# Flamingo stack on one core: order on VectorE in the first attention, seven products for half of the first values, order of values and additions in the last layer

## The chip, the cores and the metric

The kernel runs on one core of a Trainium2 chip. The core has five engines with a queue of instructions each: TensorE (PE in the profile: matrix products into PSUM; PEld is its loading of weights), VectorE (DVE), ScalarE (ACT), GpSimd (POOL) and SyncE (SP, which here issues DMAs). An engine works through its queue in order; between engines, semaphores order the work. The metric is the device time of one execution in microseconds. A measurement of this kernel can tell changes of about 0.5%.

## The reference

Four layers over x (2 batches of 256 tokens, width 256) with a context ctx (2 batches of 512 rows, width 256). Each layer adds a gated cross attention and a gated feed-forward network (FFN). What this change touches:

```python
x = x + tanh(g_xattn[0]) * L0_xattn(layernorm(x), ctx)      # softmax attention, 16 heads, no weights
x = x + tanh(g_ffn[0])   * L0_ffn(layernorm(x), W_up, W_gate, W_down)
x = x + tanh(g_xattn[1]) * L1_xattn(layernorm(x), ctx, Wq, Wk, Wv, Wo)
...
x = x + tanh(g_xattn[3]) * L3_xattn(layernorm(x), ctx, mask)
x = x + tanh(g_ffn[3])   * L3_ffn(layernorm(x), ...)        # router, top 2 of 8 experts with capacity, plus a shared MLP

def ternary_quant(w):                                       # the weights of L0_ffn
    scale = mean(abs(w)) + 1e-8
    return clip(round(w / scale), -1, 1) * scale
# L0_ffn: (silu(x @ Wu.T) * (x @ Wg.T)) @ Wd.T
# L1_xattn: v = ctx @ Wv, and so q and k; softmax(q k / sqrt(128)) v @ Wo
```

## The kernel before

All of it is one function, `flamingo`, over tiles of 128 partitions. Tokens come as four tiles n = 0..3 of 128, two of each batch. The tile framework gives each engine a queue and puts in the semaphores. It may set an instruction ahead of another one of the text; `inline` forbids that where the text's order is wanted. While the list `line` holds something, each VectorE instruction passed to `inline` stands behind the one before it; `pool_line` and `pe_line` do the same for GpSimd and TensorE. `behind(i, j, ...)` sets one instruction behind another on the same engine.

*First attention* (L442 to 550). A loop over s = 0..17 issues scores of step s and values of step s - 1: four steps for each token tile, that is two halves of the heads (i) by two halves of the context. After the values of a half of the heads, `l0_join` multiplies the result by a column of ones and zeros into `mixed` (i = 0, L473) or adds it there (i = 1, L475). When a tile is complete, TensorE exchanges neighbouring groups of 16 rows (`l0_exchange`, L479), and `l0_finish` makes the reciprocal (L485), divides and adds to x; `norm_stats` and `norm_apply` (L217 to L236) prepare the norm for the FFN, with two small GpSimd steps for the scale (L219, L220).

Between these stand parts of the ternary quantisation of the FFN's three matrices: `ternary_sum` (L339, the sum of magnitudes on VectorE), `ternary_scale`, `ternary_below` (L360, GpSimd, w < -scale/2), and `ternary_signs` (L367, VectorE, two halves of 1024 columns for each matrix). Before, the sum of the third matrix follows tile 0's statistics (step 6), and the signs of the three matrices follow the first join of tiles 1, 2 and 3 (steps 6, 10 and 14), each ahead of the second join of the same tile.

*First FFN* (`ternary_ffn`, L770). `norm_tiles(split, xn0)` transposes the four normalised tiles into PSUM buffers of the tag "tr" (there are two), and `split` takes each apart into an upper part (L778, L779) and a rest (L780). Eight chunks of the hidden width follow: for each, eight products with signs (gate and up, L277, two PSUM buffers of the tag "mm", of which there are four), silu on ScalarE (L804), a multiplication and a truncation on VectorE (L805, L372), the rest on GpSimd (L374), and, one chunk later, the product with the third matrix (`l0_down`, L793).

*Values of the next attention.* `l1_values_of(0, tiles)` (L558) multiplies each of eight tiles of context rows (four of each batch) with the value weights of the first group of four heads. Seven of them stand between the first attention and the FFN, the eighth behind `norm_tiles`. The other three groups use `seven_values`: two products of 2 x 2 blocks each with seven in place of eight block products. `batch_sums` (sums of context blocks over both batches) and `weight_sums` (sums of weight blocks) are made on GpSimd; `seven` (L604) is a generator that yields after the second, fourth and seventh product, each in an "mm" buffer or, for m1, m6, m7 and m4, a "tr" buffer; its additions are VectorE's, the copy of m1 ScalarE's. `next` on such a generator puts a part of it between other work; the loop over the heads does so.

*After the FFN* come the keys of the first two heads, the norm for the second attention, its transposes, and the heads.

*Last layer.* `l3_values(n, ...)` (four products) for each token tile, then its statistics; `l3_rows(n)` writes the normalised rows (L1544, VectorE) for the experts, and `l3_turned2(n)` transposes them (L1550) for the router's logits. GpSimd then scatters rows to the experts' slots (L1607), SyncE loads the slots (L1681), and the experts run (L1700, L1722).

*End.* `accs` are the products of the shared MLP, `rows` the routed results; `add_to_x` (L280) adds an `acc` times the gate, L1807 the rows, and `store` writes a tile (L1792).

Of the kernel before, what the change touches and what calls it, by code (L numbers as in the profile page):

```python
# [17 lines left out]
F32 = mybir.dt.float32  # L18
# [4 lines left out]
ALU = mybir.AluOpType  # L23
# [26 lines left out]
def flamingo(ctx: ExitStack, tc: tile.TileContext, a: dict, out: bass.AP):  # L50
# [202 lines left out]
    def tokens(t, n):  # L253
        return t[:, n // 2, :, n % 2 * P : (n % 2 + 1) * P]
# [105 lines left out]
            inline(nc.gpsimd.tensor_scalar(t, wi, sc[:, 2:3], None, ALU.is_lt), pool_line)  # L360
            below.append((wi, sc, t))

    def ternary_signs():
        for _ in range(2):
            wi, sc, t = below.popleft()
            signs.append(q4.tile([P, 1024], F32R, tag="q4", name="signs"))
            inline(nc.vector.scalar_tensor_tensor(signs[-1], wi, sc[:, 1:2], t, ALU.is_gt, ALU.subtract))  # L367

    def halves(hi, lo, v):

# [126 lines left out]
    for s in range(18):  # L497
        n = s // 4
        if s < 16:
            es[s] = l0_scores(n, s // 2 % 2, s % 2)  # L500
        if s < 2:

            in_turn(nc.tensor.matmul(busy, lhsT=ones, rhs=ones, start=True, stop=True))

        if s % 4 == 2 and n or s == 17:
            done = n - 1
            l0_exchange(mixed[done], acc[done, 1], done == 1)
        if 1 <= s <= 16:
            m, i, half = (s - 1) // 4, (s - 1) // 2 % 2, (s - 1) % 2
            if half == 0:  # L510
                acc[m, i] = ps_acc.tile([P, 2, D], F32, tag="acc", name="acc")
            l0_values(m, i, half, es.pop(s - 1), acc[m, i][:, 0, :])
        if s == 0:
            ternary_sum(l0_w[0])
            ternary_sum(l0_w[1])
        if s == 3:
            behind(nc.scalar.activation(tg, graw, AF.Tanh), exps[-3], "with the table of exponentials")
            p = acc[0, 0][:, 1, :]
            for w in range(2):
                in_turn(ternary_total(p[:, w : w + 1], w))  # L520
            for w in range(2):
                ternary_scale(p[:, w : w + 1])
            ternary_below(0)
            value_columns(1)
            queries([2], rest[:1])
        if s % 4 == 2 and n or s == 17:
            r = l0_finish(done, acc[done, 1], mixed[done], done == 1)
            stats[done] = norm_stats(done)
            if done == 0:
                ternary_sum(l0_w[2])  # L530
            inline(nc.gpsimd.tensor_add(all_t, all_t, sums.pop(0)), pool_line)
# [42 lines left out]
        return kT  # L574


    v_next = l1_values_of(0, range(7))

# [15 lines left out]
    def weight_sums(pool, tag, u, v):  # L594

        cols = u.shape[2]
        t = pool.tile([P, 4, cols], F32, tag=tag, name="wsum")
        nc.gpsimd.tensor_add(t[:, 0, :], v[:, 0, :], v[:, 1, :])
        nc.gpsimd.tensor_sub(t[:, 1, :], t[:, 0, :], u[:, 0, :])
        nc.gpsimd.tensor_sub(t[:, 2, :], u[:, 0, :], v[:, 0, :])  # L600
        nc.gpsimd.tensor_sub(t[:, 3, :], u[:, 1, :], t[:, 1, :])
        return t

    def seven(u, v_, s, ctx_of, product, view, out):  # L604
# [24 lines left out]
        m4 = one(v_, t4, True)  # L629
        nc.vector.tensor_add(c21, c21, m4)  # L630
        yield
# [55 lines left out]
    def seven_values(g):  # L687

        v = slab[:, 8 + 2 * (g % 2) : 10 + 2 * (g % 2), :].rearrange("p s (m c) -> p (s m) c", m=4)
        w = l1_w[g][2]  # L690
        u, z = (w[:, :, i * 256 : (i + 1) * 256] for i in range(2))
        s = weight_sums(q4, "q4", u, z)

        def product(dst, w, t):
            for j in range(2):
                nc.tensor.matmul(dst[:, j, :], lhsT=t[:, j * P : (j + 1) * P], rhs=w, start=True, stop=True)  # L696

        def two(m):
            return seven([u[:, k, :] for k in range(2)], z[:, 1, :], [s[:, i, :] for i in range(4)],
                         context_of(slice(2 * m * P, 2 * (m + 1) * P)), product, lambda t: t.rearrange("p (j c) -> p j c", j=2),  # L700
                         [[v[:, b * 4 + 2 * m : b * 4 + 2 * m + 2, i * 256 : (i + 1) * 256] for b in range(B)] for i in range(2)])

        return v, [two(m) for m in range(2)]

# [66 lines left out]
    def ternary_ffn():  # L771


        xs = [q4.tile([P, B, 2, 256], F32R, tag="q4", name="xs") for _ in range(2)]

        def split(n, tr):
            top = q1.tile([P, 2, P], F32, tag="q1", name="topx")
            nc.vector.tensor_scalar(top.bitcast(I32), tr.bitcast(I32), -4096, None, ALU.bitwise_and)  # L778
            nc.scalar.copy(tokens(xs[0], n), top)  # L779
            nc.vector.tensor_sub(tokens(xs[1], n), tr, top)  # L780

        norm_tiles(split, xn0)
        l1_values_of(0, [7])
        s2 = small.tile([P, 1], F32, tag="s2", name="s2", bufs=1)
        nc.vector.tensor_mul(s2, scales[1], scales[2])
        nc.vector.tensor_mul(s2, s2, gf(0))
# [7 lines left out]
                                     start=(c == 0 and i == 0), stop=(c == 7 and i == 1))  # L794

        ps = {}
        for c, _, ts in by_batch(FCH):
            if c not in ps:
                ps[c] = mm(), mm()
            for w, p in zip((0, 2), ps[c]):  # L800
                chain(p[:, ts], [(signs[w + k][:, c * P : (c + 1) * P], batch(h, k, ts)) for k in range(2) for h in xs])
            if ts.stop == T:
                s = q2.tile([P, T], F32, tag="q2", name="silu")
                nc.scalar.activation(s, ps[c][0], AF.Silu, scale=scales[0])  # L804
                nc.vector.tensor_mul(s, s, ps[c][1])  # L805
                h = q4.tile([P, 2, T], F32R, tag="q4", name="hT")
                halves(h[:, 0, :], h[:, 1, :], s)
                later(lambda c=c, h=h: l0_down(c, h), 1)
        flush()
        for dh in range(2):  # L810
            p = outs[dh]
# [22 lines left out]
    norm_tiles(lambda n, tr: nc.scalar.copy(tokens(xT, n), tr), xn)  # L834
# [69 lines left out]
    for g in range(4):  # L904
# [3 lines left out]
        for hl in range(4):  # L908
# [15 lines left out]
            for b in range(B):  # L924
                es, by_ones, t = l1_scores(b, qT, kT, h > 13)
                if todo:
                    next(todo)
                if extra and (h == 1 or h and b != h % 2):
                    next(extra)
                later(lambda b=b, hl=hl, v=v, es=es, by_ones=by_ones, t=t, oT=oT: l1_attend(b, hl, v, es, by_ones, t, oT), 1)  # L930
            if todo:
                next(todo)
# [626 lines left out]
    for b in range(B):  # L1559
# [242 lines left out]
    final(1)  # L1802
    store(1)
    for n in (2, 3):
        if n == 3:
            add_to_x(3, accs[1], gf(3))
        inline(nc.vector.tensor_add(x[:, n, :], x[:, n, :], rows[n][:, 0, :]))  # L1807
        store(n)
    line.clear()
    pe_line.clear()  # L1810
# [655 lines left out]
```

## Time and profile before

| | us |
|---|---|
| median of 3 runs | 573.84 |
| the three runs | 573.16, 573.84, 576.12 |
| profiled execution | 572.92 |
| its span, first to last instruction | 571.2 |

| stretch of the span (us) | what runs | PE busy | DVE busy | ACT busy | POOL busy |
|---|---|---|---|---|---|
| 20 to 28 | first attention | 8.00 | 7.36 | 6.59 | 7.32 |
| 28 to 36 | first attention | 6.30 | 7.43 | 5.44 | 7.54 |
| 36 to 44 | first attention | 8.00 | 7.53 | 6.70 | 5.76 |
| 44 to 53 | its end | 7.27 | 8.58 | 3.58 | 8.92 |
| 53 to 66 | values, transposes | 13.00 | 5.80 | 4.75 | 6.76 |
| 66 to 89 | first FFN | 23.00 | 11.05 | 12.08 | 10.35 |
| 94 to 98 | norm, transposes | 3.09 | 3.20 | 2.10 | 3.77 |

The granted TensorE clock was 0.999 of full speed. A matrix product in fp32 appears in the trace as two TensorE instructions; their ends are modelled and overlap, so the cost of a run of them is read from the distance of their starts. A line of the view of waits names engine, instruction and line, what was waited for, the sum of the waits in us, how many, and the longest. A line of the timeline has start, busy time, engine, line, operation, output and inputs, count, and in brackets the idle time before it with what ended it. A line of the chain has start, length, engine, output and line.

### The profile page before, as it was taken

How to read it: one execution, taken by the hardware profiler on the slowest of the kernel's cores; microseconds unless marked ns; L12 is line 12 of the kernel's file. 1: busy time of each engine (PE TensorE's matmuls, PEld its weight loads, DVE VectorE, ACT ScalarE, POOL GpSimd, SP SyncE). 2: the span in 40 equal slices, each digit the busy share in tenths (PEclk: the TensorE clock that was granted, in tenths of full speed). 3: DMA queues.
4: the chain of work that ended last, by engine and by line, in shares of the span. 5: the costliest groups of instructions: out<-in, count | busy, mean ns of one | idle time of the engine just before them, and what ended most of it. 6: DMA issues, size and time to landing. Idle time of an engine off the chain costs nothing.

```text
span 571.2 us, 8750 instructions
## 1 busy us (share of the span) xinstructions
PE 553.1 (97%) x3300; PEld 401.0 (70%) x3300; DVE 371.9 (65%) x744; ACT 178.7 (31%) x329; POOL 216.4 (38%) x368
## 2 busy tenths in 40 slices
PE   8988999999999999999999999999999999999996
PEld 6553675778788787887878786887775555884445
DVE  6998444677867888588885895675567434563323
ACT  5874543422222222123222221331323221432221
POOL 3787456626332464134342344702022001252151
PEclk9999999999999999999999999999999999999999
DMA  7904200002002100102032324272020899704013
GB/s 294 412 18 188 107 0 1 0 1 74 1 0 75 43 32 1 37 37 75 0 118 104 117 94 158 75 239 75 0 75 2 338 419 415 170 33 129 18 53 116
DMA packets 15528, 59.15 MB, mean 104 GB/s; under 512 B 2653, under 2 KB 5924, under 8 KB 11846
## 3 DMA queue, kind: packets, MB, share of 16 engines
q1 hardware_dynamic: 13430, 53.70, 25.7%
q0 software_dynamic: 1472, 4.28, 2.3%
q8 instruction: 28, 0.46, 0.3%
q10 hardware_dynamic: 576, 0.53, 0.3%
q14 instruction: 22, 0.18, 0.1%
HBM read 53.70 MB, written 5.25 MB: 103 GB/s over the span
## 4 chain that ended last, share of the span: by engine, by line
PE 84%; DVE 8%; POOL 3%; issue 2%; ACT 1%; DMA 1%; SPq 0%; POOLq 0%; DVEq 0%; ACTq 0%
PE mm L277 22%; PE acc L277 18%; PE mm_t L646 4%; PE mm L658 4%; PE mm L1369 4%; PE mm_t L696 4%; PE mm L646 3%; PE mm_t L658 3%; PE mm L696 3%; PE acc L766 2%; PE s L450 2%; PE mm L1700 2%; PE acc L1390 2%; PE acc L1722 2%; PE acc L464 2%
## 5 line engine op out<-in xcount | busy, mean ns | idle before, releaser
L854 ACT ACTIVATE e<-mm 128x512 f32<-128x512 f32 x64 | 38.0, 597 | 115.0 <-PE mm L277 112.4
L873 DVE RECIPROCAL r<-acc 128x256 f32<-128x256 f32 x32 | 56.2, 1757 | 20.7 <-PE acc L277 20.7
L277 PE MATMUL mm<-qT,kT 128*128 128x256 f32 x256 | 61.1, 380 | 0.0
L277 PE MATMUL acc<-e,slab 128*128 128x256 f32 x256 | 60.5, 379 | 0.0
L277 PEld LDWEIGHTS acc<-e,slab 128*128 128x128 f32 x256 | 48.6, 190 | 9.2 <-issue 2.9
L875 POOL TENSOR_TENSOR all_t<-all_t,t 128x256 f32<-128x256 f32 x32 | 24.1, 753 | 80.4 <-DVE t L859 80.4
L277 PEld LDWEIGHTS mm<-qT,kT 128*128 128x128 f32 x256 | 47.7, 190 | 9.4 <-issue 2.9
L876 POOL TENSOR_TENSOR all_r<-all_r,r 128x256 f32<-128x256 f32 x32 | 23.3, 728 | 56.4 <-DVE r L873 56.4
L277 PE MATMUL mm<-xT,slab 128*128 128x256 f32 (+1 forms) x132 | 38.7, 442 | 0.3 <-DVE k L998 0.3
L456 ACT ACTIVATE slab<-s 128x1024 f32<-128x1024 f32 x32 | 30.9, 1021 | 8.5 <-PE s L450 7.9
L858 DVE TENSOR_TENSOR t<-e,e 128x512 f32<-128x512 f32 x32 | 22.9, 716 | 15.0 <-ACT e L854 14.4
L219 POOL TENSOR_TENSOR rstd<-mv,eps_ln 128x1 f32<-128x1 f32 x26 | 6.4, 245 | 68.0 <-DVE mv L218 68.0
L277 PEld LDWEIGHTS mm<-xT,slab 128*128 128x128 f32 x132 | 24.2, 190 | 10.4 <-issue 7.1
L277 PE MATMUL acc<-slab,oT 128*128 128x256 f32 x128 | 29.4, 381 | 0.5 <-DVE oT L874 0.4
L277 PE MATMUL mm<-slab,ctxT 128*128 128x512 f32 x64 | 29.0, 594 | 0.0
L280 DVE SCALAR_TENSOR_TENSOR x<-acc,tg,x 128x256 f32<-128x256 f32 x28 | 13.5, 481 | 23.6 <-PE acc L277 19.8
L277 PEld LDWEIGHTS acc<-slab,oT 128*128 128x128 f32 x128 | 23.7, 190 | 4.9 <-DVE oT L874 1.2
L864 ACT CAST th<-t 128x256 fp32r<-128x256 f32 x28 | 11.3, 405 | 45.4 <-DVE t L862 45.4
L1369 PE MATMUL mm<-slab,xsT 128*32 128x512 f32 x192 | 22.8, 596 | 0.2 <-ACT xsT L1324 0.2
L865 POOL TENSOR_TENSOR th<-t 128x256 fp32r<-128x256 f32 x28 | 20.5, 732 | 5.6 <-DVE t L862 4.6
L236 DVE TENSOR_SCALAR xn<-x,mv,rstd 128x256 f32<-128x256 f32 x28 | 14.0, 507 | 10.4 <-POOL rstd L220 10.0
L450 PE MATMUL s<-slab,ctx_nat 32*128 32x256 f32 x256 | 20.2, 401 | 0.1
(405 smaller groups left out, 1172.2 us busy)
## 6 DMA issues: line engine op xcount, KB each, us to landing
slab<-in_l_gu_all SPq DMA_DIRECT2D x16, 1024.0 KB, 5.2
slab<-in_l_all SPq DMA_DIRECT2D x4, 2048.0 KB, 10.5
slab<-in_l_dn_all SPq DMA_DIRECT2D x4, 1024.0 KB, 5.1
slab<-in_l_dn_all SPq DMA_DIRECT2D x8, 512.0 KB, 10.0
slab<-in_l_gu SPq DMA_DIRECT2D x4, 704.0 KB, 12.5
ctx_nat<-in_ctx SPq DMA_DIRECT2D x4, 512.0 KB, 8.0
slab<-in_l_up SPq DMA_DIRECT2D x2, 1024.0 KB
slab<-in_l_gate SPq DMA_DIRECT2D x2, 1024.0 KB, 10.3
```

The lines of the kernel that those rows point to most:

```text
L277: inline(nc.tensor.matmul(dst, lhsT=lhsT, rhs=rhs, start=(i == 0), stop=(i == len(pairs) - 1)), pe_line)
L450: in_turn(nc.tensor.matmul(ps[j // 2][:, j % 2, k, :], lhsT=ctx_nat[rows, b, hf, c * P : (c + 1) * P], rhs=qm[rows, n, i, :], start=True, ...
L456: exps.append(nc.scalar.activation(es[d].rearrange("p j k q -> p (j k q)"), ps[d].rearrange("p j k q -> p (j k q)"), AF.Exp))
L646: nc.tensor.matmul(dst, lhsT=w, rhs=t, start=True, stop=True)
L658: nc.tensor.matmul(t[:, i, :], lhsT=w, rhs=b, start=True, stop=True)
L696: nc.tensor.matmul(dst[:, j, :], lhsT=t[:, j * P : (j + 1) * P], rhs=w, start=True, stop=True)
L854: nc.scalar.activation(e, s, AF.Exp, scale=HD ** -0.5)
L858: nc.vector.tensor_add(t, es[0], es[1])
L873: nc.vector.reciprocal(r, acc[:, 1, :])
L875: nc.gpsimd.tensor_add(all_t, all_t, t)
L876: nc.gpsimd.tensor_add(all_r, all_r, r)
L1369: inline(nc.tensor.matmul(ps[j * BLK : (j + 1) * BLK, :], lhsT=xsT[k][:, (4 * q + j) * BLK : (4 * q + j + 1) * BLK], rhs=gu2[:, home(q, j) ...
```

## The change

- First attention: the third matrix's `ternary_sum` moves behind tile 1's first join (step 6). The first matrix's two signs move to step 10 (behind tile 2's first join); of the second matrix's two, one moves to step 16 (behind tile 3's second join), one behind the last norm; the third matrix's two move into `ternary_ffn`, behind the last `split`.
- Values of the first group: tiles 0, 1, 4 and 5 as before; tiles 2, 3, 6 and 7 by `seven_values(0)`. Its first two products stand between the FFN's transposes (m1 in an "mm" buffer, as `in_tr` is false), m6 and m5 before chunk 4, the other three before chunk 6. Its weight sums go to two tiles of the pool q2, on GpSimd between the context sums. The products and the chunks are held in the text's order on TensorE.
- Second group of values: the first part of its generator (two products, one copy, one addition) is issued with the second attention's transposes; the loop over heads has one part fewer to take.
- Last layer: `l3_turned2(0)` stays behind the values of tile 2, `l3_turned2(1)` goes behind those of tile 3.
- End: for tile 3 the routed rows are added before the shared MLP's product.

```diff
-    def ternary_signs():
-        for _ in range(2):
+    def ternary_signs(halves, last=None):
+        for _ in range(halves):
             wi, sc, t = below.popleft()
             signs.append(q4.tile([P, 1024], F32R, tag="q4", name="signs"))
-            inline(nc.vector.scalar_tensor_tensor(signs[-1], wi, sc[:, 1:2], t, ALU.is_gt, ALU.subtract))
+            i = inline(nc.vector.scalar_tensor_tensor(signs[-1], wi, sc[:, 1:2], t, ALU.is_gt, ALU.subtract))
+            if last:
+                behind(i, last[0], "the norm is waited for")
...
             stats[done] = norm_stats(done)
-            if done == 0:
-                ternary_sum(l0_w[2])
...
                 rest = [norm_stats(m) for m in (2, 3)]
-            else:
-                ternary_signs()
+            elif n == 1:
+                ternary_sum(l0_w[2])
+            elif n == 2:
+                ternary_signs(2)
         if s % 4 == 0 and s:
...
                 norm_apply(n - 2, xn0, stats[n - 2])
+            if n == 4:
+                ternary_signs(1)
     norm_apply(3, xn0, stats[3])
+    ternary_signs(1)
...
-    v_next = l1_values_of(0, range(7))
+    v_next = l1_values_of(0, (0, 1, 4, 5))
...
+    def sums_into(t, u, v):
+        behind(nc.gpsimd.tensor_add(t[0], v[:, 0, :], v[:, 1, :]), l0_pool, "not among the first attention's")
+        nc.gpsimd.tensor_sub(t[1], t[0], u[:, 0, :])
+        behind(nc.gpsimd.tensor_sub(t[2], u[:, 0, :], v[:, 0, :]), l0_pool, "not among the first attention's")
+        nc.gpsimd.tensor_sub(t[3], u[:, 1, :], t[1])
...
-        m1 = one(u[0], b0, True)
+        m1 = one(u[0], b0, in_tr)
...
-        s = weight_sums(q4, "q4", u, z)
+        if g:
+            s = weight_sums(q4, "q4", u, z)
+            s = [s[:, i, :] for i in range(4)]
+        else:
+            s = [t[:, i, :] for t in (q2.tile([P, 2, 256], F32, tag="q2", name="wsum") for _ in range(2)) for i in range(2)]
+            sums_into(s, u, z)
 
         def product(dst, w, t):
             for j in range(2):
-                nc.tensor.matmul(dst[:, j, :], lhsT=t[:, j * P : (j + 1) * P], rhs=w, start=True, stop=True)
+                inline(nc.tensor.matmul(dst[:, j, :], lhsT=t[:, j * P : (j + 1) * P], rhs=w, start=True, stop=True), pe_line)
...
-            nc.vector.tensor_sub(tokens(xs[1], n), tr, top)
-
+            last_split[:] = [nc.vector.tensor_sub(tokens(xs[1], n), tr, top)]
+
+        values = seven_values(0)[1][1]
         norm_tiles(split, xn0)
-        l1_values_of(0, [7])
+        next(values)
+        ternary_signs(2, last_split)
...
+        pe_line.append(None)
         for c, _, ts in by_batch(FCH):
+            if c in (4, 6):
+                next(values)
...
     values_of[1], sets_of[1] = seven_values(1)
+    next(sets_of[1][0])
...
                 if todo:
-                    next(todo)
+                    next(todo, None)
...
-            if n == 2:
-                for m in range(2):
-                    l3_turned2(m)
+            if n > 1:
+                l3_turned2(n - 2)
...
     for n in (2, 3):
+        inline(nc.vector.tensor_add(x[:, n, :], x[:, n, :], rows[n][:, 0, :]))
         if n == 3:
             add_to_x(3, accs[1], gf(3))
-        inline(nc.vector.tensor_add(x[:, n, :], x[:, n, :], rows[n][:, 0, :]))
         store(n)
```

More of the change, by code (lines that the diff above doesn't have):

```diff
@@ L597, in weight_sums, with seven @@
         t = pool.tile([P, 4, cols], F32, tag=tag, name="wsum")
[L598 to L601, printed above, removed]
-        return t
-    def seven(u, v_, s, ctx_of, product, view, out):
+        sums_into([t[:, i, :] for i in range(4)], u, v)
+        return t
+    def sums_into(t, u, v):
[3 more added lines that the diff above has]
+        nc.gpsimd.tensor_sub(t[3], u[:, 1, :], t[1])
+    def seven(u, v_, s, ctx_of, product, view, out, in_tr=True):
         b0, b0_, b1, b1_, t1, t2, t3, t4 = ctx_of
@@ L691, in seven_values @@
         u, z = (w[:, :, i * 256 : (i + 1) * 256] for i in range(2))
-        s = weight_sums(q4, "q4", u, z)
+        if g:
[4 more added lines that the diff above has]
+            sums_into(s, u, z)
         def product(dst, w, t):
             for j in range(2):
-                nc.tensor.matmul(dst[:, j, :], lhsT=t[:, j * P : (j + 1) * P], rhs=w, start=True, stop=True)
+                inline(nc.tensor.matmul(dst[:, j, :], lhsT=t[:, j * P : (j + 1) * P], rhs=w, start=True, stop=True), pe_line)
         def two(m):
-            return seven([u[:, k, :] for k in range(2)], z[:, 1, :], [s[:, i, :] for i in range(4)],
+            return seven([u[:, k, :] for k in range(2)], z[:, 1, :], s,
                          context_of(slice(2 * m * P, 2 * (m + 1) * P)), product, lambda t: t.rearrange("p (j c) -> p j c", j=2),
-                         [[v[:, b * 4 + 2 * m : b * 4 + 2 * m + 2, i * 256 : (i + 1) * 256] for b in range(B)] for i in range(2)])
+                         [[v[:, b * 4 + 2 * m : b * 4 + 2 * m + 2, i * 256 : (i + 1) * 256] for b in range(B)] for i in range(2)], g > 0)
         return v, [two(m) for m in range(2)]
@@ L774, in ternary_ffn @@
         xs = [q4.tile([P, B, 2, 256], F32R, tag="q4", name="xs") for _ in range(2)]
+        last_split = []
         def split(n, tr):
@@ L808, in ternary_ffn @@
                 later(lambda c=c, h=h: l0_down(c, h), 1)
+        pe_line.clear()
         flush()
@@ L931, in flamingo @@
             if todo:
-                next(todo)
+                next(todo, None)
             if extra and (h == 1 or h and h % 2 == 0):
```

## The prediction

> **What bounds the kernel now.** First the page's table of engines: TensorE (PE) is busy for nearly the whole span, so a change pays only where it takes work from TensorE or fills one of its few waits.
>
> ```profile
> span 571.2 us, 8750 instructions
> PE 553.1 (97%) x3300; PEld 401.0 (70%) x3300; DVE 371.9 (65%) x744; ACT 178.7 (31%) x329; POOL 216.4 (38%) x368
> ```
>
> Then the view of waits, asked for TensorE alone in the first 110 us: who was waited for, the sum, how often, the longest.
>
> ```profile
> PE acc L479 <- DVE mixed L475: 2.5, 2, 1.3
> PE tr L248 <- ACT xT L834: 0.6, 1, 0.6
> PE acc L464 <- DVE mixed L473: 0.4, 1, 0.4
> PE tr L248 <- DVE xn L236: 0.3, 1, 0.3
> ```
>
> The two largest stand in the first attention: the exchange (L479) waits for the join (L475). VectorE's (DVE's) timeline shows what was in front of the joins: the ternary signs, and the sum of the third matrix's magnitudes.
>
> ```profile
> 27.08 2.25 DVE L339 TENSOR_REDUCE tq_part<-slab 128x1 f32<-128x2048 f32 x1
> 30.03 2.80 DVE L367 SCALAR_TENSOR_TENSOR signs<-slab,tq_sc,tern 128x1024 fp32r<-128x1024 f32 x2
> 33.67 0.70 PE L479 MATMUL acc<-mixed,swap 128*128 128x256 f32 x2 [1.27 <-DVE mixed L475]
> 48.35 3.09 DVE L367 SCALAR_TENSOR_TENSOR signs<-slab,tq_sc,tern 128x1024 fp32r<-128x1024 f32 x2
> 52.28 0.70 PE L479 MATMUL acc<-mixed,swap 128*128 128x256 f32 x2 [1.27 <-DVE mixed L475]
> ```
>
> The chain that ended last gives the later places: TensorE from 52.98 to the FFN at 65.88 without a gap, the transposes of the last layer's first half, and the two additions after the last product.
>
> ```profile
> 52.98 10.30 PE mm L277 x24
> 63.28 0.44 PE tr L248 x4
> 63.72 1.72 PE mm L277 x4
> 65.44 0.44 PE tr L248 x4
> ...
> 500.94 0.82 DVE slab L1544
> 501.75 0.14 issue
> 501.89 0.41 PE tr L1550 x2
> ...
> 565.97 0.50 DVE x L280
> 566.47 0.03 DVEq L1807
> 566.50 0.04 issue
> 566.54 0.43 DVE x L1807
> ```
>
> **The change, part by part.** Durations are from this execution. "Built order" is the order in which the changed program places its instructions on an engine, and what each waits for; it has no times.
>
> *First attention on VectorE.* No sum and no sign stands before the joins that were late. The join before values step 9 now comes right after the statistics (end 27.2), so the wait of 0.4 goes. The sum (2.25) and the second join (0.86) then end at 31.2; the exchange is due at 33.67 - 1.27 - 0.4 = 32.0, so its 1.27 goes. The third exchange keeps its two signs ahead of the join; all of it moves together. At the last exchange no sign is left in front: the wait of 1.27 goes. Together **-2.9**, and the last exchange starts at 49.3.
>
> *Values.* A tile of 128 context rows costs four TensorE instructions, 24 in 10.30 us, so 0.43 each and 1.72 a tile. Half of the eight (6.88) become seven products of the width 256, which the chain shows at 0.86 each: 6.02. **-0.86**. The additions (seven on VectorE at 0.69, one copy on ScalarE) and four weight sums on POOL (0.73 each) lie beside TensorE's work, if they are in time.
>
> *New wait at the transposes.* From the last exchange on TensorE needs 0.7 + three tiles 5.16 + two tiles' transposes 0.44 + six instructions of the first two products (1.29), to 56.9. The built order has the next transposes wait for the split (topx, xs) of the first two, since there are two buffers for them. VectorE: join to 48.3, norm 0.56, one sign 1.5 (the group's mean is 1.512) to 50.4; the reciprocal up to the end of the last norm took 53.02 to 58.19, 5.2, to 55.6; another sign to 57.1; then the split, whose first results come 1.0 and 1.4 later: 58.1 and 58.5. TensorE waits 56.9 to 58.1 and a little again: **+1.5**. Least 0.6 (the two signs at the fastest row, 1.27 each, and the norm at 0.42), most 2.8 (signs at 1.9, the slowest, and 0.5 where POOL's scale comes late: its two steps took 1.17 and 1.50 beside a sign at 49.13, 0.19 and 0.55 alone at 56.52).
>
> *New wait in the FFN.* It would start at 59.3 (transposes 0.44, the product's rest 0.43) instead of 65.88. VectorE goes on: second pair of splits to 60.0, one addition 0.69, the last two signs 2.9 to 63.6, then the first multiplication 0.69 and the truncation 0.43 to 64.8, then POOL's 1.30 to 66.1. Queued behind those two signs is the multiplication, for it wait the second product of chunk 2 (its bank) and POOL's lower half, and for that the first outT product. It stood 71.61 - 65.88 = 5.7 after the FFN's start, so is due at 65.0 and comes some 1.1 late: **+1.2**. Least 0; most 2.7, because POOL too has more to do: from 54.7 on two running sums 1.5, three context sums at 1.27, four weight sums 0.73 and 0.6 of small things end at 63.6, and each of three signs can hold it for 0.9 (an addition took 1.65 beside a sign, 0.72 without):
>
> ```profile
> 38.96 1.65 POOL L531 TENSOR_TENSOR all_t<-all_t,mixed 128x256 f32<-128x256 f32 x1
> 51.84 0.72 POOL L531 TENSOR_TENSOR all_t<-all_t,mixed 128x256 f32<-128x256 f32 x1
> ```
>
> The Trainium skill, "SBUF — State Buffer", section "Who interferes with whom", speaks against this placing: a VectorE instruction with two SBUF inputs shuts out a GpSimd instruction that reads SBUF, and whichever is second stands still for all of the other. The signs have two such inputs, and they are moved to where POOL makes the sums. By that rule the wait would lie near its upper end, 2.7, and the total 1.5 us higher; the two rows above agree with a block, not with how often it would fall here, so I keep the 1.2.
>
> The five later products (4.3) run between the chunks. Their PSUM bank is one of four: m5 keeps it from chunk 4 to chunk 6. In the built order the second product of chunk 5 then waits for the silu of chunk 4, which by the chunk round (1.8 of products, 0.9 of outT) is over 1.5 us earlier. I put that at nothing; without this cover it is the third rival.
>
> *The loads.* The second pair of group loads on SP's queue now waits for the last signs: 63.6 instead of 49.18. Behind it on SP stands nothing before 130.10, and the first reader of the group is a weight sum at 137.99; two loads at 10.5 from issue to landing end before 90. Nothing.
>
> *After the FFN.* Two products (0.86 each) that stood at 98.0 and 103.3 move up; one of them now stands between the two pairs of transposes, where TensorE was idle 0.58 and 0.33 by the timeline, and nearly all of 96.3 to 97.04 by the chain. With the other's whole run before the queries, the same work is 1.3 ahead at the second scores. **-1.1**: 0.6 at least (the wait for ScalarE alone), 1.4 at most.
>
> *Last layer.* The second transposition moves behind the values of tile 3. The wait of 0.8 (500.94 to 501.75 in the chain, VectorE writes the rows) is covered by these values, 1.74. The logits now come 0.44 after the values, and the copy between (0.37) lies beside the first two logits. From there the path goes over the slots to POOL's eight scatters and their landing; TensorE and these are both due at 524.3, so both must gain. **-0.5** (0.2 to 0.8).
>
> *End.* The addition of the routed rows (0.43) goes ahead of the last product's. Only one operation is left after it: **-0.5** (0.4 to 0.55).
>
> **Sum.** -2.9 - 0.86 + 1.5 + 1.2 - 1.1 - 0.5 - 0.5 = -3.2. The profiled execution took 572.92, of which its span is 571.2, so it would be 569.7. The median of the three runs is 573.84 and the lowest 573.16; the profiled one is 0.9 below the median. I put the base halfway, at 573.4, and forecast **570.2**, against which the rivals are set too. With all bounds the sum runs from -2.9 - 0.86 + 0.6 - 1.4 - 0.8 - 0.55 = -5.9 to -2.9 - 0.86 + 2.8 + 2.7 - 0.6 - 0.2 - 0.4 = +0.5, so 567.5 to 573.9.
>
> **Rivals.**
> 1. *No new wait.* The two terms of 1.5 and 1.2 vanish, as VectorE has 5.8 of 13 us busy between 53 and 66, and signs went at 1.27 at best. For it: that slack. Against it: the slack is before the transposes, the new work after the norm. -3.2 - 2.7 = -5.9: 567.5, and 566.9 with the other terms at their best.
> 2. *The first stage gives back all it gains.* POOL and VectorE block each other as bounded above, so the -3.8 are eaten, and of the -1.1 half remains: -0.5 - 0.5 - 0.5: 571.9. For it: the 1.65 row. Against it: POOL's lower half starts 63.6 at the earliest, VectorE needs it at 64.8, so there is room of 1.2.
> 3. *The bank that m5 keeps.* With three banks the chunks go in series: 1.8 of products, then silu 0.69 and multiplication 0.69, only 0.9 of it under outT, +0.5 in each of four chunks; and the seven additions (4.8) stand on VectorE in front of multiplications that are then waited for. +6.8 on the forecast: 577.0, slower. It decides from the point at which a chunk's second product starts later than 1 us after its first. Against it: the round has 1.5 us of room.
>
> **Chances.** Forecast 0.51 (two thirds of it below 570.97, which is 0.5% under the median, about what a measurement of this kernel can tell from no change), first rival 0.25, second 0.15, third 0.09. So faster by over 0.5%: 0.33 + 0.25 = 0.58; within 0.5%: 0.18 + 0.15 = 0.33; slower by over 0.5%: 0.09. The range leaves out the third rival and the upper end, where all bounds meet: 566.9 to 573.0; the forecast's own, with its two new waits moved by half the way to their bounds, is about 568.9 to 571.7.
>
> **What would show it.** In the waits of the first 110 us L479 and its 2.5 must be gone, the last exchange must start near 49.3, and the FFN's first product near 59.3, with a wait of the transposes on VectorE's split in front. Chunk 0's multiplication should start near 63.6, straight behind two signs. The outputs' transposes, 90.85 before, should come at about 89.8. The last store should follow one operation after the last product. Wrong: transposes that don't wait for the split (first rival), a lower half of chunk 0 on POOL after 67 (second), chunk rounds over 3.2 us (third), or scatters of the last layer that start no earlier against its norms than now.

## The result and the profile after

| | before | after |
|---|---|---|
| median (22 runs each) | 574.51 | 573.15 |
| ratio of times | | 0.9982, 95% interval 0.9968 to 0.9997 |
| profiled execution / its span | 572.92 / 571.2 | 573.04 / 570.8 |

A gain of some 1.0 to 1.4 us, within what counts as no change; a second comparison, among the experiments, gave 0.9979 (0.996 to 0.9999). The forecast was 570.2, range 566.9 to 573.0. Runs of one program differ by up to 4.6 us, with granted clocks from 0.990 to 1.000, so what follows reads small differences from distances between places in the profiles, which repeat far better.

The table of engines: TensorE's busy time is what it was, VectorE and GpSimd have gained 6.2 and 3.5.

```profile
span 570.8 us, 8782 instructions
PE 553.0 (97%) x3312; PEld 403.9 (71%) x3312; DVE 378.1 (66%) x751; ACT 177.0 (31%) x326; POOL 219.9 (39%) x372
```

The view of waits, TensorE alone, first 112 us. The waits for joins (2.5 and 0.4) are gone; a wait at the transposes has come, and three in the FFN:

```profile
PE tr L248 <- DVE xs L795: 2.0, 1, 2.0
...
PE outT L811 <- POOL hT L376: 0.7, 1, 0.7
...
PE mm L277 <- DVE silu L826: 0.4, 1, 0.4
...
PE outT L811 <- ACT hT L375: 0.2, 1, 0.2
```

TensorE's timeline has them in their places. The last exchange starts at 49.38 (before 52.28) and the FFN at 59.72 (before 65.63); the second outT instruction stands at 68.33:

```profile
49.38 0.59 PE L481 MATMUL acc<-mixed,swap 128*128 128x256 f32 x2
...
58.90 0.74 PE L248 MATMUL tr<-ident,xn 128*128 128x128 f32 x4 [2.03 <-DVE xs L795]
...
59.72 5.34 PE L277 MATMUL mm<-xs,signs 128*128 128x256 f32 x36
65.51 1.42 PE L277 MATMUL mm<-xs,signs 128*128 128x512 f32 x5 [0.45 <-DVE silu L826]
...
68.33 0.96 PE L811 MATMUL outT<-hT,signs 128*128 128x512 f32 x3 [0.71 <-POOL hT L376]
```

The chain that ended last says what was late. Before, it ran on TensorE alone from 52.98 to the FFN; now it goes over VectorE's signs and reciprocal and then over GpSimd's sums:

```profile
49.34 1.67 DVE signs L367
51.01 1.68 DVE r L487
...
56.67 2.21 POOL ctx_nat L594
...
61.51 2.27 POOL ctx_nat L597
63.78 1.67 POOL wsum L609
...
67.01 1.28 POOL hT L376
68.33 0.96 PE outT L811 x3
```

VectorE's and GpSimd's timelines, laid beside each other, show why. The four signs (L367) behind the last join take 1.75, 1.75 and, the last two together, 3.51 (singly 1.28 and 2.32); two signs with nothing of GpSimd's beside them take 2.47 together (the kernel with the values as before, below). Each context or weight sum that starts beside a sign takes 1.0 longer than the same sum free of signs (L595 1.28, L610 0.73). The sign of 1.28 met a sum that was over 0.17 later (L608); the one of 2.32 met L597, itself held by the sign before, with 1.24 still to run:

```profile
49.26 1.75 DVE L367 SCALAR_TENSOR_TENSOR signs<-slab,tq_sc,tern 128x1024 fp32r<-128x1024 f32 x1
...
56.01 1.75 DVE L367 SCALAR_TENSOR_TENSOR signs<-slab,tq_sc,tern 128x1024 fp32r<-128x1024 f32 x1
...
61.34 3.51 DVE L367 SCALAR_TENSOR_TENSOR signs<-slab,tq_sc,tern 128x1024 fp32r<-128x1024 f32 x2
64.78 0.68 DVE L826 TENSOR_TENSOR silu<-silu,mm 128x512 f32<-128x512 f32 x1
```

```profile
56.63 2.25 POOL L594 TENSOR_TENSOR ctx_nat<-ctxT 128x512 f32<-128x512 f32 x1
...
59.52 1.28 POOL L595 TENSOR_TENSOR ctx_nat<-ctxT,ctx_nat 128x512 f32<-128x512 f32 x1
60.77 0.74 POOL L608 TENSOR_TENSOR wsum<-wsum,slab 128x256 f32<-128x256 f32 x1
61.47 2.31 POOL L597 TENSOR_TENSOR ctx_nat<-ctxT,ctx_nat 128x512 f32<-128x512 f32 x1
63.73 1.71 POOL L609 TENSOR_TENSOR wsum<-slab 128x256 f32<-128x256 f32 x1
65.40 0.73 POOL L610 TENSOR_TENSOR wsum<-slab,wsum 128x256 f32<-128x256 f32 x1
```

Where the time went, as distances between places in TensorE's timeline. "Stage" is the distance from the first exchange, which no edit touches, to the output transposes of the FFN; "loss" is the stage less the kernel before's.

| kernel | to the last exchange | to the FFN | stage | loss |
|---|---|---|---|---|
| before | 29.61 | 42.96 | 68.02 | |
| after | 26.56 | 36.90 | 68.88 | +0.86 |

The places that the table rests on and that are not shown yet, before and then after:

```profile
22.67 0.70 PE L479 MATMUL acc<-mixed,swap 128*128 128x256 f32 x2
...
65.63 6.14 PE L277 MATMUL mm<-xs,signs 128*128 128x256 f32 x41
...
90.69 1.03 PE L816 MATMUL tr<-ident,o 128*128 128x128 f32 x8
```

```profile
22.82 0.70 PE L481 MATMUL acc<-mixed,swap 128*128 128x256 f32 x2
...
91.70 1.04 PE L838 MATMUL tr<-ident,o 128*128 128x128 f32 x8
```

So the first stage gained 3.05 at the last exchange and 6.06 at the FFN's start, and had lost everything and 0.86 more at its end. Behind it the change gains: from the output transposes to the next attention's second query product (111.57 and 111.50), up to which both kernels have the same work to do, it is 20.88 before and 19.80 after, -1.08; from the last layer's first transposition (500.74 and 500.38) to the count of good rows (the product into `good`, at 524.16 and 523.12) 23.42 and 22.74, -0.68. The first transposition now runs ahead of tile 3's values, the second behind them, without a wait:

```profile
500.38 0.38 PE L1573 MATMUL tr<-ident,slab 128*128 128x128 f32 x2
500.60 1.89 PE L277 MATMUL acc<-ctx_nat,e 128*128 128x256 f32 x8
502.33 0.38 PE L1573 MATMUL tr<-ident,slab 128*128 128x128 f32 x2
```

At the end only one operation stands behind the routed rows' additions, but it ends 42.63 after the count of good rows, against 42.81 before: 0.2. What lies between it and the end of the span took 5.05, against 4.23.

### The profile page after: what moved, and what is told of

Same layout as the page of the kernel before. It is cut to its first block, busy times and chain, and to the rows that moved or that the text cites. A ratio compares the mean times of both kernels' runs of the same rounds, so it can differ in the third digit from the quotient of the medians.

```text
span 570.8 us, 8782 instructions
## 1 busy us (share of the span) xinstructions
PE 553.0 (97%) x3312; PEld 403.9 (71%) x3312; DVE 378.1 (66%) x751; ACT 177.0 (31%) x326; POOL 219.9 (39%) x372
## 4 chain that ended last, share of the span: by engine, by line
PE 81%; DVE 6%; POOL 5%; DMA 3%; issue 3%; ACT 1%; SPq 0%; POOLq 0%; DVEq 0%; ACTq 0%
PE mm L277 19%; PE acc L277 18%; PE mm_t L654 4%; PE mm_t L709 4%; PE mm L666 4%; PE mm L1392 4%; PE mm L654 3%; PE mm_t L666 3%; PE mm L709 3%; PE s L452 2%; PE acc L779 2%; PE mm L1722 2%; PE acc L466 2%; PE acc L1413 2%; DMA slab<-in_l_gate 2%
## 5 line engine op out<-in xcount | busy, mean ns | idle before, releaser
L881 DVE TENSOR_TENSOR t<-e,e 128x512 f32<-128x512 f32 x32 | 22.9, 716 | 14.6 <-ACT e L877 14.1
L277 PE MATMUL mm<-slab,ctxT 128*128 128x512 f32 x48 | 22.0, 595 | 0.0
```

The source lines that it names most:

```text
L277: inline(nc.tensor.matmul(dst, lhsT=lhsT, rhs=rhs, start=(i == 0), stop=(i == len(pairs) - 1)), pe_line)
L881: nc.vector.tensor_add(t, es[0], es[1])
```

## The experiments

Times are medians; "ratio" is against the kernel before on the same chip. The stages of all kernels stand together behind the last experiment.

### Which queue holds the FFN's first chunk

The first four take the changed kernel apart. **The last sign goes behind chunk 3** (`halves` now returns its truncation, behind which the sign is set):

```diff
-        ternary_signs(2, last_split)
+        ternary_signs(1, last_split)
...
+                top = halves(h[:, 0, :], h[:, 1, :], s)
+                if c == 3:
+                    ternary_signs(1, [top])
```

> The second sign of the third matrix goes from in front of chunk 0's multiplication to behind chunk 3's truncation; nothing else moves. In the changed kernel that multiplication starts at 64.78, the first lower half on GpSimd at 67.01 and the output transposes at 91.86. Theory (VectorE's queue and GpSimd's list both hold the first chunk, GpSimd's list ends last): the multiplication starts at 63.4, one block of a GpSimd sum by a sign (1.0) goes, the lower half starts at 66.0, the output transposes at 90.9, and the kernel gains 1.0. Rival 1 (VectorE's order alone): a gain of 1.4. Rival 2 (the stall is not of VectorE or GpSimd but of PSUM banks or the silu): no gain.

Measured 573.34, ratio 0.9972 (0.9954 to 0.999). The stage is 67.94, 0.94 shorter than after's. The multiplication came 14.1 behind the last exchange, against 15.4, and the wait for it is gone. The view of waits of this kernel (TensorE, 16 to 98) still has the one for GpSimd, so GpSimd's list ends last, as the theory has it:

```profile
PE tr L248 <- DVE xs L796: 2.0, 1, 2.0
PE outT L812 <- POOL hT L376: 1.1, 1, 1.1
```

**Two of GpSimd's sums go into its idle time before the last statistics** (in the loop at step 16, behind the sign; they are left out where they stood):

```diff
+                inline(nc.gpsimd.tensor_sub(early[:, 0, :], ctxT[:, 1, 0, :], ctxT[:, 0, 0, :]), pool_line)
+                inline(nc.gpsimd.tensor_add(wsum0[0][:, 0, :], w0[:, 0, 256:512], w0[:, 1, 256:512]), pool_line)
```

> One context sum and one weight sum (2.0 on GpSimd) go into GpSimd's idle time before the last statistics (49.9 to 54.4); the signs stay. Theory (both queues): GpSimd's list is done by 65, the lower half of chunk 0 then waits for VectorE's truncation and starts at 66.4 in place of 67.01: a gain of 0.6. Rival 1 (VectorE's order alone): no gain. Rival 2 (GpSimd's list alone): a gain of 2.0.

572.67, ratio 0.9963 (0.9949 to 0.9978). The stage is 67.38, 1.50 shorter: more than the 0.6 expected. The edit was to leave VectorE alone, and did not: with fewer sums beside them the two signs before chunk 0 took 2.96 in place of 3.51, so the multiplication came earlier too. The block works in both directions. VectorE's timeline of this kernel:

```profile
61.05 2.96 DVE L367 SCALAR_TENSOR_TENSOR signs<-slab,tq_sc,tern 128x1024 fp32r<-128x1024 f32 x2
63.93 0.68 DVE L833 TENSOR_TENSOR silu<-silu,mm 128x512 f32<-128x512 f32 x1
```

**Both edits:**

> The edits of the two before it together. Theory (both queues): multiplication at 63.4, truncation done at 64.9, lower half at 64.9 in place of 67.01, output transposes at 89.8: a gain of 2.1, more than the 1.6 of the two alone. Rival 1 (VectorE's order alone): 1.4 as with the sign alone. Rival 2 (GpSimd's list alone): 3.0.

571.74, ratio 0.995 (0.9931 to 0.9969). The stage is 66.57: 2.31 shorter, near the 2.1. It is not more than the two alone add up to (2.44), as the second one had already helped VectorE. TensorE waits for nothing in the FFN any more; the 2.0 at the transposes stay. VectorE alone (1.4) and GpSimd alone (3.0) are both out.

**The second matrix's last sign goes behind the split of tiles 0 and 1:**

```diff
-    ternary_signs(1)
...
+            if n == 1:
+                ternary_signs(1, last_split)
```

> The second sign of the second matrix goes from in front of the first split to behind the split of tiles 0 and 1; nothing else moves. Theory (the wait at the transposes and the one in the FFN are one and the same backlog of VectorE, seen twice): the wait of 2.0 at the transposes falls to 0.4 and the FFN starts at 58.1 in place of 59.72, but chunk 0's multiplication stays at 64.8, since VectorE has the same work in front of it; the output transposes stay at 91.9 and the time within 0.3. Rival (two separate waits): a gain of 1.6.

574.02, ratio 1.0001 (0.9981 to 1.0022). The FFN starts 1.65 earlier, and the stage is 68.84, as good as after's 68.88. The time was expected within 0.3 of the changed kernel's; the median is 0.8 above it, on another chip, and the interval is too wide to decide. The view of waits has the 2.0 spread over others:

```profile
PE mm L277 <- DVE slab L624: 0.9, 1, 0.9
PE mm L277 <- DVE silu L827: 0.9, 1, 0.9
PE outT L812 <- POOL hT L376: 0.7, 1, 0.7
...
PE tr L248 <- DVE xs L794: 0.4, 1, 0.4
```

So the wait at the transposes and the stall in the FFN are one backlog of VectorE (and of GpSimd behind it). What is taken off it in one place is paid in the next, as long as the same work stands in front of chunk 0's multiplication.

### Which part of the change makes the backlog

**The changed kernel again**, as the reference of its chip:

> The changed kernel once more, unaltered, beside the three that follow, so that positions and times are compared on one chip. Expected: 1.0 to 1.4 below the kernel before; last exchange 49.4, output transposes 91.7. In the runs so far the last row that is scattered left GpSimd 30.7 after the count of good rows in the changed kernel and 32.4 in the others. If that is the chip, it is 32.4 here too and the last addition comes later; if it is the programs, it is 30.7.

573.27, ratio 0.9979 (0.996 to 0.9999); stage 68.89. The last scatter left GpSimd at 555.52, 32.0 after the count (523.51): the same program that had 30.7 in its first profile. So it is not the programs. In the experiments it goes with the chip, as far as one profile of each kernel shows: 32.3 to 32.4 in all four kernels of the chip of the first four experiments, 31.5 to 32.2 in the four of this chip, 30.7 in the four of the last one.

**The first values as before the change,** signs as the change has them:

```diff
-    v_next = l1_values_of(0, (0, 1, 4, 5))
+    v_next = l1_values_of(0, range(7))
...
-        values = seven_values(0)[1][1]
         norm_tiles(split, xn0)
-        next(values)
+        l1_values_of(0, [7])
```

> All eight first values as four plain products a tile, seven tiles before the FFN and one between its transposes, as before the change; the signs stay where the change puts them. TensorE has 0.86 more work, but VectorE has 3.4 more time before the FFN, and GpSimd has no weight sums. Theory (the seven products take away the cover of VectorE's signs): no wait at the transposes, chunk 0's multiplication at most 0.8 late, output transposes at 88.3 in place of 91.7: 3.4 less than the changed kernel. Rival (the sign order itself makes the backlog, wherever the products are): both waits stay and it is 0.9 slower than the changed kernel.

569.69, ratio 0.9916 (0.9887 to 0.9945), 3.6 below the changed kernel beside it. The stage is 65.28, 3.60 shorter than after's, 2.74 shorter than the kernel before's. The signs stand in the same order, but now VectorE is done before TensorE's transposes come, as its timeline in this kernel shows: the split waits 2.87 for TensorE, where in the changed kernel TensorE waited for the split. The last two signs go at 1.24 each, with no weight sums on GpSimd beside them.

```profile
55.57 1.74 DVE L367 SCALAR_TENSOR_TENSOR signs<-slab,tq_sc,tern 128x1024 fp32r<-128x1024 f32 x1
60.17 0.75 DVE L793 TENSOR_SCALAR topx<-tr 128x256 int32<-128x256 int32 x2 [2.87 <-PE tr L248]
...
63.59 2.47 DVE L367 SCALAR_TENSOR_TENSOR signs<-slab,tq_sc,tern 128x1024 fp32r<-128x1024 f32 x2
65.98 0.68 DVE L822 TENSOR_TENSOR silu<-silu,mm 128x512 f32<-128x512 f32 x1
```

**The seven products, with the signs spread** over VectorE's gaps (the first at step 8, one fewer behind the last norm), and the edits of the third experiment:

```diff
                 norm_apply(n - 2, xn0, stats[n - 2])
+            if n == 2:
+                ternary_signs(1)
...
     norm_apply(3, xn0, stats[3])
-    ternary_signs(1)
```

> The seven products stay; the signs are spread into VectorE's gaps: the first behind tile 0's norm (idle 1.73 there), two at step 10, the fourth at step 16, the fifth behind the last split, the sixth behind chunk 3; one context sum and one weight sum into GpSimd's gap. Theory (a backlog of VectorE and GpSimd is all that the first stage lost): wait at the transposes 0.4, stall in the FFN below 0.3, output transposes at 87.4 in place of 91.7: 4.2 less than the changed kernel. Rival (the five products among the chunks cost of themselves, through PSUM banks or additions): output transposes not before 88.5.

569.72, ratio 0.9918 (0.9887 to 0.9949). Stage 64.92, 3.96 shorter; in the view of waits a wait of 0.4 at the transposes is all that is left of the backlog:

```profile
PE tr L248 <- DVE xs L804: 0.4, 1, 0.4
PE tr L248 <- DVE xn L236: 0.2, 1, 0.2
```

**The later edits alone** (the kernel before with the second group's first part, the last layer's and the end's order):

> The kernel before with the later edits alone: first part of the second group's values beside the second attention's transposes, the last layer's order, the end's order. Theory (from the changed kernel's trace): query product 1.2 earlier, logits 0.7 more, end 0 to 0.5: 2.0 below the kernel before. Rival (the norm gap and the last layer are given back later, by loads or scatters): less than 1.0.

573.08, ratio 0.9976 (0.9955 to 0.9998): some 1.4, with the theory's 2.0 and the rival's 1.0 both inside the interval, so the places decide. Its stage is 68.03, the next distance 19.82, and last layer and end are as in the changed kernel: nothing is given back before the end.

**The seven products, with the sum and the signs where they stood before:**

```diff
+            if done == 0:
+                ternary_sum(l0_w[2])
...
-            elif n == 1:
-                ternary_sum(l0_w[2])
-            elif n == 2:
+            else:
                 ternary_signs(2)
```

> The changed kernel with the sum and the signs where they stood before the change; the seven products and the later edits stay. With the run that has the new signs and the old values (569.69) and the later edits alone (573.08) this closes the square. Theory (the two parts compete for the same time of VectorE after the last exchange): the last exchange is back at 52.3, no wait at the transposes and no stall in the FFN, the stage is 0.5 shorter than before the change, 572.5. Rival (the products among the chunks cost of themselves): 574 or more.

572.77, ratio 0.9969 (0.9949 to 0.9989). The joins are waited for again (2.6), the transposes not; the FFN starts 5.2 earlier than before the change, but the stage is 68.07, not 0.5 shorter. This closes the square (stage):

| | signs as before | signs as changed |
|---|---|---|
| values as before | 68.02, 68.03 | 65.28 |
| half of them by seven products | 68.07 | 68.88, 68.89 |

The sign order alone gains 2.7, the seven products alone nothing, and both together lose 0.9.

### The end

**The spread signs with the end's old order:**

> The kernel with the spread signs (569.72), with the end's order as before the change: for tile 3 the shared MLP's product first, the routed rows last. Theory (the end edit pays 0.5 only where TensorE's last product ends last; where the last scatter leaves GpSimd 32 after the count of good rows, the routed rows end last and the new order costs an addition): 0.5 below the kernel with the spread signs if the last scatter is late, 0.5 above it if it is at 30.7. Rival (TensorE's product ends last in any case): 0.5 above it.

**The spread signs with more buffers for the experts' outputs** (every second one from the pool of large tiles):

```diff
-        o = q1.tile([P, D], F32, tag="q1", name="o3")
+        o = q4.tile([P, 4, D], F32, tag="q4", name="o3")[:, 0, :] if q % 2 else q1.tile([P, D], F32, tag="q1", name="o3")
```

> The kernel with the spread signs, with more buffers for the experts' outputs: every second one in the pool of large tiles, so that the last copy waits for the scatter of block 3 and not of block 5. Theory (the last copy stood still for the landing of an earlier scatter): the last scatter leaves GpSimd 30.7 or less after the count of good rows, the last addition waits for TensorE's last product, and the time is 0.5 to 1.2 below the kernel with the spread signs. Rival (the landing of the last scatter and of the loads behind it sets the end): less than 0.3.

570.83 (ratio 0.9937, 0.9913 to 0.9961) and 569.95 (0.9922, 0.9894 to 0.995). Neither decides what it was made for. The last scatter left at 30.7 in both, and in the other kernel of that chip with the old buffers (the seven products with old signs) as well, so the late scatter did not occur and the buffers had nothing to mend; that the last copy stands still for an earlier scatter's landing stays argued. The end's order can be read: with the old one the last VectorE operation ends 42.82 after the count of good rows, with the new one, in the three others on that chip, 42.43 to 42.65. The new order gains 0.2 to 0.4, not 0.5, where the last scatter leaves at 30.7: routed rows and TensorE's last product come at nearly the same time, and VectorE goes from one addition to the next without a wait for TensorE. On the two chips where the scatter leaves later all eight kernels have the new order, and the last operation ends 42.76 to 44.04 after the count; what the order is worth there, no run shows. VectorE's timeline of the kernel with more buffers has two additions of rows, then the product's, and no bracket of idle time at either:

```profile
562.43 0.75 DVE L1838 TENSOR_TENSOR x<-x,o3g 128x256 f32<-128x256 f32 x2
563.28 0.48 DVE L280 SCALAR_TENSOR_TENSOR x<-acc,tg,x 128x256 f32<-128x256 f32 x1
```

**A version that puts together what paid:** old values, last sign behind chunk 3, more buffers.

> The changed kernel with the first values as before the change, its last sign behind chunk 3, and more buffers for the experts' outputs. Theory: 0.4 for the sign that stood before chunk 0's multiplication (FFN start to output transposes 25.1 in place of 25.5), 0.5 to 1.2 at the end: 568.4 to 568.8, below both kernels of the case. Rival (the end is set by landings): 569.3.

568.77, ratio 0.9917 (0.9885 to 0.9949). Below both kernels of the case, and not to be told from the values as before alone (0.9916). The sign behind chunk 3 did harm here: chunk 0's multiplication came 0.4 sooner than with the values as before alone, as expected, but the stage is 65.66, 0.38 longer, since that sign held the lower half of chunk 3 on GpSimd (2.17 in place of 1.30) and no products stood between the chunks to cover it, as they do in the kernels with the seven (with the spread signs the same lower half took 2.18, and TensorE did not wait). From its timeline, VectorE, GpSimd and TensorE:

```profile
73.58 1.28 DVE L367 SCALAR_TENSOR_TENSOR signs<-slab,tq_sc,tern 128x1024 fp32r<-128x1024 f32 x1
73.84 2.17 POOL L376 TENSOR_TENSOR hT<-silu,top 128x512 fp32r<-128x512 f32 x1 [1.71 <-DVE top L374]
...
76.06 0.96 PE L811 MATMUL outT<-hT,signs 128*128 128x512 f32 x3 [0.70 <-POOL hT L376]
```

| kernel | to the FFN | stage | against before |
|---|---|---|---|
| last sign behind chunk 3 | 36.89 | 67.94 | -0.08 |
| two sums early | 36.89 | 67.38 | -0.64 |
| both | 36.89 | 66.57 | -1.45 |
| sign behind the split | 35.24 | 68.84 | +0.82 |
| values as before | 39.81 | 65.28 | -2.74 |
| spread signs (three kernels) | 35.22 to 35.25 | 64.92 to 64.96 | -3.1 |
| seven products, old signs | 37.74 | 68.07 | +0.05 |
| old values, last sign behind chunk 3 | 39.80 | 65.66 | -2.36 |

## Why the prediction was wrong

The miss is 2.95: 573.15 against 570.2. Of it 1.1 is the **base**: I put it at 573.4, from three runs and a profile; the median of 22 is 574.5. The rest, 1.8, is the sum: -3.2 forecast, -1.4 by the medians. Step by step:

- *First attention, -2.9.* Right: -3.05.
- *Values, -0.86.* Right as TensorE's work. From the last exchange to the FFN it took 13.35 before and 8.23 with seven products and old signs, 5.1 less (forecast 6.88 - 1.72 = 5.16). The five products among the chunks, in the kernel with the spread signs, take 1.54 and 2.40 from start to start, and lengthen two rounds by 0.2 each: 4.36 (forecast 4.3). That is -0.8. But with the old signs the stage did not get shorter by it: the FFN's instructions up to the first outT took 6.33 in place of 5.98, outT waited 0.28, and some 0.3 I can't place.
- *New wait at the transposes, +1.5.* Mechanism right, size off: 2.03. I took one sign at the group's mean, 1.5; beside GpSimd's additions it took 1.75, and two stand in front.
- *New wait in the FFN, +1.2.* **This step failed**: it is 2.6 (31.98 from the FFN's start to the output transposes, less 25.06 before and 4.36 for the five products). Of it, 2.3 goes with the two edits of the third experiment. I let GpSimd's list end at 63.6 and kept its blocks for the upper bound, "each of three signs can hold it for 0.9". They came every time, 1.0 each, and the list ended at 66.9; on VectorE the multiplication came at 64.78, not 63.6, as the four signs took 7.0 and not 5.9. (The truncation behind it took 0.93 and not 0.43, but was done at 66.42, before GpSimd's list.) The due time was also set too early: the 5.7 to the first outT took its end from the timeline and its start from the chain. By either alone it is 5.9 to 6.0, and the term would have been 0.8 to 0.9. The Trainium skill's rule ("SBUF — State Buffer", "Who interferes with whom"), that a VectorE instruction with two SBUF inputs and a GpSimd instruction reading SBUF exclude each other, was the better guide: it would have put this term at 2.7. I had the row for it (1.65 beside a sign, 0.72 without) and weighed it as a matter of chance; but in the order as built, signs and sums were both back to back in that place, and two full queues must meet. The rule did not hold for every pair, though: GpSimd's comparison (L360), which reads SBUF, had 1.17 still to run when a sign of the kernel with the spread signs started, and that sign took 1.28 all the same.
- *Two terms for one backlog.* I gave the two waits bounds apart. The sign behind the split shows them to be one: the work in front of chunk 0's multiplication decides, wherever TensorE meets it first. The miss does not come from this, as the forecast itself carried VectorE's queue on from the one to the other.
- *The bank that m5 keeps, the loads: nothing.* Right: chunk rounds in the chain are 2.75 (74.53 to 77.28) with m5 in its bank; no wait for a load came.
- *After the FFN, -1.1.* Right: -1.08, in every kernel that has the edit.
- *Last layer, -0.5 (0.2 to 0.8).* -0.68.
- *End, -0.5 (0.4 to 0.55).* Off: 0.2 to 0.4 at the last operation, and what follows it varied from 4.23 to 5.75 between profiles, so it can't be seen in the time.

With the measured terms, -3.05 - 0.8 + 2.0 + 2.6 - 1.1 - 0.7 - 0.3 = -1.35; with the first stage as measured as a whole, +0.86, it is -1.2. The medians have -1.4, the ratio -1.0.

Of the rivals it was the second, "the first stage gives back all it gains", that came, and somewhat more than all; its sign, a lower half of chunk 0 on GpSimd after 67, came at 67.01. That its total of -1.5 is near the measured -1.4 is in part luck: the stage lost 0.86 more than it gained, and the gain behind the FFN, which the rival halved, stayed whole. I gave it 0.15 on account of a room of 1.2 between GpSimd's end and VectorE's truncation; the room was reckoned with GpSimd unhindered, just what the rival denied. The first and the third are out: there were new waits, and the chunks did not go in series.

## What to carry to other kernels

A part that takes work off the bounding engine also takes away the cover of what the other engines do in that time: add up the queue of each of them up to the next hand-over, and charge one backlog once, not each wait for itself. Two edits that each pay or cost nothing alone can lose together when they use the same slack; take the square of both before adding gains. Where VectorE's signs and GpSimd's sums were both back to back, one stood still for the other every time; price two full queues so, and VectorE's instructions with one SBUF operand too, as the truncation shows.

## What the runs showed of the hardware

- A sign (two SBUF operands, 128x1024) takes 1.27 or 1.28 with no GpSimd instruction beside it, and no more where a GpSimd sum had 0.25 or less still to run as it started. With 0.66 still to run it took 1.74 or 1.75, with 1.24 it took 2.32. The GpSimd instruction that starts beside a sign with 1.0 or more of it left takes 0.9 to 1.0 more, whatever its own size (1.27 to 2.25, 0.73 to 1.71, 1.30 to 2.17).
- Not every pair does so. In the kernel with the spread signs the sign at 30.62 started with 1.17 of GpSimd's comparison (L360, 128x1024) still to run, and they took 1.28 and 2.85, as each does alone. In the kernel before, a sign that started with 2.26 of that comparison to run took 1.60.
- One SBUF operand is not always safe, and two operands with one in PSUM were. VectorE's truncation (128x512, one operand, in SBUF) takes 0.43 in the changed kernel with GpSimd idle (72.70), and 0.93, 1.52 and 1.03 where a GpSimd instruction had 0.65, 1.23 and 0.74 still to run (65.49, 67.05, 69.19). VectorE's multiplication of the same chunks, with one operand in PSUM, left GpSimd alone: in the changed kernel it ran from 68.48, GpSimd's lower half from 68.64, and they took 0.68 and 1.30 as elsewhere.
- Distances in the first stage repeat to 0.04 over several chips (the last exchange 26.56 or 26.57 behind the first in all eleven profiles with the new sign order), while the first exchange itself starts anywhere from 22.33 to 23.17, and the end of the span lies 4.2 to 5.8 behind the last VectorE operation. Two profiles of one program can't show a gain of 0.5 in their spans.
- The changed kernel let its last scatter go 30.7 after the count of good rows in its first profile and 32.0 in its second. In the experiments it goes with the chip: the four profiles of a chip agreed to 0.05 on two chips and to 0.7 on the third. The chip of the first profile is not on record, and what in a chip would do it, no run shows.
